# Transposing attention probabilities through DRAM: partition-wise writes and four sorted reads in place of four sorted writes and partition-wide reads

## The chip, the cores and the metric

The kernel is one program on one core of a Trainium2 chip. The metric is the device time of one execution in microseconds, given as the median of several runs. A profiled execution of the same program gives the trace that is read here. The core's engines are named as the profile names them: PE (TensorE; PEld is its weight load), DVE (VectorE), ACT (ScalarE), POOL (GpSimd) and SP (SyncE). DMAs are issued from the queues of SP, ACT and POOL.

## The reference, cut to what matters

All data are 32-bit floats. There are 8 sequences of 128 rows of 512 numbers. Two residual blocks follow one another:

```python
x = x + lora_experts(adapter(x))        # layer 0
x = x + ffn(attention(x, kv_cache))     # layer 1
```

The attention takes most of the work. It has 32 query heads, 8 key heads (4 query heads to each), a head size of 128, and a paged cache of 16 pages of 32 rows for each sequence:

```python
q = rope(rmsnorm(x @ Wq.T)); k = rope(rmsnorm(x @ Wk.T)); v = x @ Wv.T
k_all = concat([k_cache[block_table], k]); v_all = concat([v_cache[block_table], v])
scores = q @ k_all.T * SCALE            # 128 x 640 for each head
scores = where(valid, scores, -1e30)
probs  = softmax(scores)
out    = (probs @ v_all) @ Wo.T
```

The product of probabilities and values needs the probabilities transposed: keys on the partitions, queries along the row. The queries and keys of the scores need a transposition too: the head's 128 numbers on the partitions.

## The kernel before, in words

A unit is one sequence and one key head with its 4 query heads, so there are 64 units, and two neighbouring units (GH = 2) are one step: the same sequence, two key heads. The order on every engine is the order in which the program states the instructions; nothing is rearranged. After a prologue (layer 0, the first projections, tables and rotations) a loop runs `iteration(u)` for u from 0 to 66. Several units are under way in it at once. In iteration u:

- SP gathers the key pages of the next step (`gather`, L196: 32 KB each): 10 in the even iterations, 6 in the odd ones (L1245). The first three stand ahead of the read of exchange u-1 (`exchange_in`), the others behind it.
- POOL gathers values (`gather_v`, L206), and in odd iterations makes the rotation tables of a later step (`make_tables`, L235, two products).
- For each of the 4 heads PE computes the scores (L837, L840), DVE adds the mask and finds the lowest (L850), ACT takes the exponential (L861), DVE the reciprocal of the sum (L866), POOL divides (L867), and DVE turns 32 x 32 blocks of the result into the tile `pb` (`blocks`, L872). At the third head DVE also turns the blocks of queries and keys of unit u+2 into the end of the same tile (`blocks_qk`, L823). PE puts output products (L1044) and projections (L261) of other units between the heads; DVE takes the projections up (L264).
- ACT then copies the queries and keys of unit u+1 out of what exchange u-1 brought (`heads_qk`, L906), takes the squares and scaled values of unit u+3 (`norms`, L310 and L312), and issues its half of the write of exchange u. POOL finishes the norms (L314, L316).
- After the four heads `exchange_out(u)` writes `pb` to DRAM (L886). `exchange_in(u)` reads it back in the next iteration (L896, L899).
- DVE rotates the queries and keys of unit u+3 (`rotate`, L328 to L346). PE multiplies probabilities and values of unit u-2 (`values`, L919).

**The exchange.** `pb` holds, on each of 128 partitions, QD = 4 pieces of XW = 800 numbers: PW = 640 of probabilities and NH * 32 = 160 of queries and keys. The turn of 32 x 32 blocks has transposed within the blocks. What is left is to move block (i, k) to (k, i), where i and k count the four groups of 32 partitions and the four pieces of a row; this goes through the DRAM tile `px`. Before the change the sorting is done by the writes. There are four, one for each group i of 32 partitions, in the order of the groups: the first two on SP's queue, the others on ACT's. Each writes pieces of 3200 bytes to their sorted places. Then two reads on SP's queue bring whole rows of DRAM into all 128 partitions: queries and keys (`qkb`) first, then the probabilities (`pT`). The tile `pb` has one buffer, `pT` two, `qkb` one. Units 0 and 1 use the `pT` buffers for their `pb`, which have no room for queries; those of unit 1 are put into a gap of `xo` and written in four DMAs of their own.

The two halves of the movement, as they stand:

```python
m = dram_x.tile([QD, 32, QD, XW], F32, tag="px", name=f"px_{u}")
...
out=m[:, :, i, n:end].rearrange("k b f -> b k f"),
in_=src[i * 32 : (i + 1) * 32],
...
nc.sync.dma_start(out=qkb, in_=m[:, :, PW:])
...
nc.sync.dma_start(out=pT, in_=m[:, :, :PW])
```

The functions that the diff touches, with what calls them, follow.

Of the kernel before, what the change touches and what calls it, by code (L numbers as in the profile page):

```python
# [9 lines left out]
F32 = mybir.dt.float32  # L10
I32 = mybir.dt.int32
AF = mybir.ActivationFunctionType
# [4 lines left out]
P = 128  # L17
B = 8
S = 128
# [4 lines left out]
D = 128  # L24
HKV, REP = 8, 4
NH = REP + 1
PAGES, PSIZE, NPP = 64, 32, 16
# [3 lines left out]
GH = 2  # L31
NQ = HKV // GH
HW = NH // 2 * D + D
QD = P // 32
HN = DM // 2
PW = REP * (LC + 1) * 32
XW = PW + NH * 32
# [21 lines left out]
def adaln_ffn_kernel(  # L59
# [25 lines left out]
    nc = tc.nc  # L85
# [33 lines left out]
        out=nw, in_=norm_w.rearrange("o (t d) -> o t d", t=2).to_broadcast([P, 2, D])  # L119
# [15 lines left out]
    xo = keep.tile([P, B // 2, 7, 2, S], F32, name="xo")  # L135
# [90 lines left out]
    NU = len(units)  # L226
    rs_t, qk_t, vn_t, tab_t, c_t, part_t = {}, {}, {}, {}, {}, {}

    def make_tables(st):

        b = st % B
        t = pj.tile([P, 2, 4, D // 2], F32, tag="tab", name=f"tab_{st}", bufs=2)
        nwv = nw.rearrange("p i (t d) -> p (i t) d", t=2)
        for i, f in enumerate((cos, sin)):
            nc.gpsimd.tensor_tensor(  # L235
                t[:, i], nwv, f[:, b, :].unsqueeze(1).to_broadcast([P, 4, D // 2]), ALU.mult
            )
        tab_t[st] = t
# [64 lines left out]
    def norms(u):  # L303

        cs, b = c_t[u], units[u][0] % B
        ss = pj.tile([P, NH], F32, tag="ss", name=f"ss_{u}", bufs=5)
        sq = pj.tile([P, D], F32, tag="sq", name=f"sq_{u}")
        for h in range(NH):
            at = h // 2 * HW + h % 2 * D if h < REP else 2 * D
            nc.scalar.activation(sq, cs[:, at : at + D], AF.Square, accum_out=ss[:, h : h + 1])  # L310
        vn = pj.tile([P, D], F32, tag="vn", name=f"vn_{u}", bufs=6)
        nc.scalar.activation(vn, cs[:, 2 * HW - D :], AF.Copy, scale=down[:, b : b + 1])  # L312
        vn_t[u] = vn
        nc.gpsimd.tensor_scalar(ss, ss, 1.0 / D, eps[:, b : b + 1], ALU.mult, ALU.add)  # L314
        rs = pj.tile([P, NH], F32, tag="rs", name=f"rs_{u}", bufs=5)
        nc.gpsimd.tensor_tensor(rs, ss, mhalf, ALU.pow)  # L316
        rs_t[u] = rs
# [31 lines left out]
    def rotate(u):  # L349
        rotate_q(u)  # L350
        rotate_k(u)
# [46 lines left out]
    with ExitStack() as l0:  # L398
# [217 lines left out]
        for t in range(B):  # L616
# [31 lines left out]
                l0_angles(t - 1)  # L648
            if t in (3, 6):
                gather_v(t // 3 - 1, 0, LC)  # L650
            if t in (5, 6):
                make_tables(t - 5)
            if t == 4:
                project_whole(0, 0, 0, 0)
            if t == 5:
# [12 lines left out]
        project_whole(0, 1, 1, 0)  # L668
        l0_turn(B - 2)
        rotate(1)  # L670
        l0_experts(B - 1)
        project_whole(1, 0, 0, 0)
        transpose_qk(1)
# [117 lines left out]
    with ExitStack() as l1:  # L791
# [6 lines left out]
        )  # L798

        p_t, pb_t, pT_t, den_t, o_t, oT_t, y_t = {}, {}, {}, {}, {}, {}, {}  # L800
        mask_t, px_t, qkb_t, qk_out = {}, {}, {}, {}

        def make_mask(st):
            b = st % B
# [4 lines left out]
        def new_pb(u):  # L809

            if u < 2:
                pb_t[u] = wk1.tile([P, QD, PW], F32, tag=f"pT{u}", name=f"pb_{u}")
                return
            pb_t[u] = wk1.tile([P, QD, XW], F32, tag="pb", name=f"pb_{u}")

        def blocks_qk(u, w):

            if w == 1:
                gap = xo[:, 0, 4:].rearrange("p x c s -> p (x c s)")[:, : NH * S]
                qk_out[w] = gap.rearrange("p (i f) -> p i f", i=QD)  # L820
            else:
                qk_out[w] = pb_t[w][:, :, PW:]
            nc.vector.transpose(  # L823
                qk_out[w].rearrange("p i (h a) -> p h i a", a=32),
                qk_t.pop(u).rearrange("p h t d -> p h (t d)").rearrange(
                    "p h (i a) -> p h i a", a=32
                ),
            )
# [40 lines left out]
        def blocks(u, h):  # L869
# [4 lines left out]
                p_t.pop((u, h)).rearrange("p (j i a) -> p j i a", i=QD, a=32),  # L874
            )

        def exchange_out(u):

            pb = pb_t.pop(u)
            m = dram_x.tile([QD, 32, QD, XW], F32, tag="px", name=f"px_{u}")  # L880
            w = XW if u + 2 in range(3, NU) else PW
            for i in range(QD):
                eng = nc.sync if i < QD // 2 else nc.scalar
                for n, end in ((PW, w), (0, PW)) if u == 1 else ((0, w),):
                    src = qk_out[u] if n else pb[:, :, :end]
                    (nc.sync if n else eng).dma_start(  # L886
                        out=m[:, :, i, n:end].rearrange("k b f -> b k f"),
                        in_=src[i * 32 : (i + 1) * 32],
                    )
            px_t[u] = m  # L890

        def exchange_in(u):
            m = px_t.pop(u).rearrange("k b i f -> (k b) i f")
            if u + 2 in range(3, NU):
                qkb = wk1.tile([P, QD, NH * 32], F32, tag="qkb", name=f"qkb_{u + 2}")
                nc.sync.dma_start(out=qkb, in_=m[:, :, PW:])  # L896
                qkb_t[u + 2] = qkb
            pT = wk1.tile([P, QD, PW], F32, tag=f"pT{u % 2}", name=f"pT_{u}")
            nc.sync.dma_start(out=pT, in_=m[:, :, :PW])  # L899
            pT_t[u] = pT  # L900

        def heads_qk(u):

# [321 lines left out]
        def iteration(u):  # L1225
# [16 lines left out]
                slots = (1, 2, 6) if four else (4, 5, 3)  # L1242
            st = u // GH
            pages = on(u) and 1 < st + 1 < NQ * B
            first, end = ((0, 10), (10, NPP))[u % GH]  # L1245
            if pages:
                gather(st + 1, first, first + 3)
            if on(u - 1):
# [266 lines left out]
```

## Time and profile before

| what | value |
|---|---|
| median of 3 runs | 1235.75 us (1232.12 to 1240.6) |
| the profiled execution's own time | 1228.33 us |
| its span in the profile | 1226.5 us |
| DVE, POOL and ACT busy | 909.9, 721.2 and 503.7 us |
| DMA moved in the span | 302.71 MB, 247 GB/s on average |
| L837, scores: matmuls of 128x512 | 504, 259.2 us in all |
| L919, values: matmuls of 128x512 | 640, 295.6 us in all |
| L872, block turns of probabilities | 256, 825 ns each |
| L906, copies of queries and keys | 61, 712 ns each |
| L235, tables | 64 products, 741 to 747 ns each |

How to read the profile: times count from the start of the span. The matmuls of PE are pipelined and overlap, so the sum over a group is more than the time in which the group ran. A line of a timeline gives the start, the time taken, the engine (with a q for an engine's queue that issues DMAs), the line of the program, the operation, what it writes and reads, how many in a row, and in brackets the engine's idle time before it with what ended it. In the table of stages each number of busy us has the count of instructions in brackets behind it. A group's name such as `pT<-px` means: into the tile `pT`, from `px`.

### The profile page before, as it was taken

How to read it: one execution, taken by the hardware profiler on the slowest of the kernel's cores; microseconds unless marked ns; L12 is line 12 of the kernel's file. 1: busy time of each engine (PE TensorE's matmuls, PEld its weight loads, DVE VectorE, ACT ScalarE, POOL GpSimd, SP SyncE). 2: the span in 40 equal slices, each digit the busy share in tenths (PEclk: the TensorE clock that was granted, in tenths of full speed). 3: DMA queues.
4: the chain of work that ended last, by engine and by line, in shares of the span. 5: the costliest groups of instructions: out<-in, count | busy, mean ns of one | idle time of the engine just before them, and what ended most of it. 6: DMA issues, size and time to landing. Idle time of an engine off the chain costs nothing.

```text
span 1226.5 us, 16786 instructions
## 1 busy us (share of the span) xinstructions
PE 1202.6 (98%) x4159; PEld 709.2 (58%) x4159; DVE 909.9 (74%) x2098; ACT 503.7 (41%) x1457; POOL 721.2 (59%) x801
## 2 busy tenths in 40 slices
PE   8999989999999999999999999999999999999998
PEld 7765445565555556555556565655555555655444
DVE  2545877887988787878888787888787878876522
ACT  1344544444444444444344444444443444443211
POOL 2433868778755576677656675687556775732100
PEclk9999999999999999999999999999999999999999
DMA  8832688888888988898789888998889888888742
GB/s 306 286 101 96 205 253 251 247 272 275 261 245 251 280 259 237 294 288 287 236 263 294 281 231 270 297 289 248 246 257 287 262 255 262 263 260 235 219 126 97
DMA packets 206836, 302.71 MB, mean 247 GB/s; under 512 B 84819, under 2 KB 120404, under 8 KB 205844
## 3 DMA queue, kind: packets, MB, share of 16 engines
q1 hardware_dynamic: 174964, 208.72, 53.9%
q10 hardware_dynamic: 18720, 52.32, 15.9%
q0 software_dynamic: 13056, 40.60, 9.8%
q8 instruction: 33, 0.54, 0.2%
q14 instruction: 63, 0.52, 0.1%
HBM read 185.64 MB, written 115.93 MB: 246 GB/s over the span
## 4 chain that ended last, share of the span: by engine, by line
PE 68%; DMA 12%; DVE 6%; POOL 5%; issue 3%; SPq 3%; ACT 2%; ACTq 0%; DVEq 0%; POOLq 0%
PE o L919 15%; PE p L261 14%; PE s L837 12%; PE y L1044 10%; DMA px<-pb 9%; PE s L840 3%; PE bp L548 2%; PE op L1402 2%; DVE pb L872 2%; PE cp L526 2%; PE y L1057 2%; POOL p L867 2%; PE fz L733 2%; PE p L294 2%; POOL wqkv L166 1%
## 5 line engine op out<-in xcount | busy, mean ns | idle before, releaser
L861 ACT ACTIVATE p<-p,low 128x640 f32<-128x640 f32 x256 | 211.6, 827 | 463.1 <-DVE den L866 300.9
L867 POOL TENSOR_SCALAR p<-p,den 128x640 f32<-128x640 f32 x256 | 208.6, 815 | 270.2 <-DVE den L866 268.8
L261 PE MATMUL p<-wqkv,xo 128*128 128x384 f32 x784 | 282.3, 487 | 5.1 <-DVE c L264 4.9
L850 DVE CUSTOM_DVE_ANT_0 p<-s,mask,rs 128x640 f32<-128x640 f32 x256 | 222.0, 878 | 78.8 <-PE s L840 77.9
L837 PE MATMUL s<-kt,qkT 128*128 128x512 f32 x504 | 259.2, 596 | 8.5 <-DVE low L850 3.3
L919 PE MATMUL o<-pT,vt 128*128 128x512 f32 x512 | 230.2, 592 | 0.0
L872 DVE STREAM_TRANSPOSE pb<-p 128x640 f32<-128x640 f32 x256 | 211.0, 825 | 18.7 <-POOL p L867 18.7
L1044 PE MATMUL y<-wo,oT 128*128 128x256 f32 x784 | 206.6, 380 | 0.1
L261 PEld LDWEIGHTS p<-wqkv,xo 128*128 128x128 f32 x784 | 147.8, 190 | 75.9 <-DVE c L264 10.1
L840 PEld LDWEIGHTS s<-qkT 128*128 128x128 f32 x504 | 95.8, 190 | 120.5 <-issue 120.5
L206 POOL DMA_INDIRECT vt<-in_vc,vrow x128 | 143.3, 1120 | 33.8 <-issue 31.8
L919 PEld LDWEIGHTS o<-pT,vt 128*128 128x128 f32 x512 | 97.3, 190 | 110.3 <-issue 95.2
L837 PEld LDWEIGHTS s<-kt,qkT 128*128 128x128 f32 x504 | 93.4, 190 | 82.3 <-issue 34.3
L1044 PEld LDWEIGHTS y<-wo,oT 128*128 128x128 f32 x784 | 131.8, 191 | 8.9 <-PE s L840 0.2
L310 ACT ACTIVATE sq<-c 128x128 f32<-128x128 f32 x320 | 98.8, 309 | 8.1
L840 PE MATMUL s<-qkT 128*128 128x128 f32 x504 | 96.8, 274 | 0.0
L823 DVE STREAM_TRANSPOSE pb<-ca 128x640 f32<-128x640 f32 x60 | 50.3, 839 | 52.5 <-DMA px<-pb 51.5
L316 POOL TENSOR_TENSOR rs<-ss,mhalf 128x5 f32<-128x5 f32 x64 | 83.1, 1298 | 5.3
L942 ACT COPY oT<-o 128x512 f32<-128x512 f32 x64 | 37.5, 585 | 90.7 <-PE o L919 67.4
L919 PE MATMUL o<-pT,vn 128*128 128x512 f32 x128 | 65.4, 592 | 0.0
L314 POOL TENSOR_SCALAR ss<-ss,eps 128x5 f32<-128x5 f32 x64 | 21.6, 338 | 74.2 <-ACT sq L310 74.2
L264 DVE TENSOR_TENSOR c<-c,p 128x384 f32<-128x384 f32 x84 | 44.8, 534 | 22.5 <-PE p L261 22.4
(193 smaller groups left out, 1415.0 us busy)
## 6 DMA issues: line engine op xcount, KB each, us to landing
pT<-px SPq DMA_DIRECT2D x64, 1280.0 KB
px<-pb ACTq DMA_DIRECT2D x120, 400.0 KB
px<-pb SPq DMA_DIRECT2D x120, 400.0 KB
qkb<-px SPq DMA_DIRECT2D x61, 320.0 KB
kt<-in_kc SPq DMA_DIRECT2D x512, 32.0 KB
wqkv<-in_wqkv POOLq DMA_DIRECT2D x32, 384.0 KB, 5.3
wo<-in_wo POOLq DMA_DIRECT2D x17, 512.0 KB, 6.2
yd<-yp SPq DMA_DIRECT2D x12, 512.0 KB
```

The costliest lines, as they stand in the source:

```text
L206: nc.gpsimd.indirect_dma_start(out=kv_t[step][1][:, c, :], out_offset=None, in_=vc, in_offset=bass.IndirectOffsetOnAxis(ap=vrow[:, hf, at ...
L261: nc.tensor.matmul(out=ps, lhsT=xo[:, pr, x, c, :], rhs=w[:, c, :], start=(c == 0), stop=(c == 1))
L310: nc.scalar.activation(sq, cs[:, at : at + D], AF.Square, accum_out=ss[:, h : h + 1])
L316: nc.gpsimd.tensor_tensor(rs, ss, mhalf, ALU.pow)
L837: nc.tensor.matmul(out=s[:, :L], lhsT=qkT[:, h, :], rhs=kt[:, :, g % GH, :], start=True, stop=True)
L840: nc.tensor.matmul(out=s[:, L:NK], lhsT=qkT[:, h, :], rhs=qkT[:, REP, :], start=True, stop=True)
L850: nc.vector.tensor_tensor_reduce(out=p, in0=s_t.pop((u, h))[:, :NK], in1=mask_t[st], scale=rs_t[u][:, h : h + 1], scalar=BIG, op0=ALU.add, ...
L861: nc.scalar.activation(p, p, AF.Exp, bias=low, scale=-1.0, accum_out=den)
L867: nc.gpsimd.tensor_scalar(p_t[u, h], p_t[u, h], den, 1.0, ALU.mult, ALU.mult)
L872: nc.vector.transpose(pb_t[u][:, :, h * w : (h + 1) * w].rearrange("p i (j a) -> p j i a", a=32), p_t.pop((u, h)).rearrange("p (j i a) -> ...
L919: nc.tensor.matmul(out=o, lhsT=vt[:, c, j * D : (j + 1) * D] if c < LC else vn_t.pop(u), rhs=pT[:, c], start=(c == 0), stop=(c == LC),)
L1044: nc.tensor.matmul(out=y_t["y"][:, half * HN : (half + 1) * HN], lhsT=part(key)[:, i * S : (i + 1) * S], rhs=wo_t[:, slot(w, key[0] // (B ...
```

## The change

The writes no longer sort: two DMAs of 64 partitions each, one on SP and one on ACT, write each partition's row in one piece (12,800 bytes). The reads sort instead: four DMAs on SP's queue, one for each piece k of a row, gather that piece from all rows into the 32 partitions of group k, with the queries and keys and the probabilities together. So `qkb` is gone, and `heads_qk` reads the end of the `pT` tile, which grows to XW. Room is made by one buffer instead of two for the tables, with the second table of the prologue made after `rotate(1)`, and by letting the squares of `norms` go into `vn` in place of a tile of their own. Units 0 and 1 now have a full-sized `pb`, so unit 1's queries need no gap in `xo`. The key pages are gathered 8 and 8 instead of 10 and 6.

```diff
-        t = pj.tile([P, 2, 4, D // 2], F32, tag="tab", name=f"tab_{st}", bufs=2)
+        t = pj.tile([P, 2, 4, D // 2], F32, tag="tab", name=f"tab_{st}")
...
-        sq = pj.tile([P, D], F32, tag="sq", name=f"sq_{u}")
+        vn = pj.tile([P, D], F32, tag="vn", name=f"vn_{u}", bufs=6)
         for h in range(NH):
             at = h // 2 * HW + h % 2 * D if h < REP else 2 * D
-            nc.scalar.activation(sq, cs[:, at : at + D], AF.Square, accum_out=ss[:, h : h + 1])
-        vn = pj.tile([P, D], F32, tag="vn", name=f"vn_{u}", bufs=6)
+            nc.scalar.activation(vn, cs[:, at : at + D], AF.Square, accum_out=ss[:, h : h + 1])
...
-            if t in (5, 6):
-                make_tables(t - 5)
+            if t == 5:
+                make_tables(0)
...
         rotate(1)
+        make_tables(1)
         l0_experts(B - 1)
...
-                pb_t[u] = wk1.tile([P, QD, PW], F32, tag=f"pT{u}", name=f"pb_{u}")
+                pb_t[u] = wk1.tile([P, QD, XW], F32, tag=f"pT{u}", name=f"pb_{u}")
...
+        def width(u):
+
+            return XW if u + 2 in range(3, NU) else PW
+
         def exchange_out(u):
 
-            pb = pb_t.pop(u)
-            m = dram_x.tile([QD, 32, QD, XW], F32, tag="px", name=f"px_{u}")
-            w = XW if u + 2 in range(3, NU) else PW
-            for i in range(QD):
-                eng = nc.sync if i < QD // 2 else nc.scalar
-                for n, end in ((PW, w), (0, PW)) if u == 1 else ((0, w),):
-                    src = qk_out[u] if n else pb[:, :, :end]
-                    (nc.sync if n else eng).dma_start(
-                        out=m[:, :, i, n:end].rearrange("k b f -> b k f"),
-                        in_=src[i * 32 : (i + 1) * 32],
-                    )
+            pb, w = pb_t.pop(u), width(u)
+            m = dram_x.tile([P, QD, XW], F32, tag="px", name=f"px_{u}")
+            for eng, at in ((nc.sync, slice(0, P // 2)), (nc.scalar, slice(P // 2, P))):
+                eng.dma_start(out=m[at, :, :w], in_=pb[at, :, :w])
             px_t[u] = m
 
         def exchange_in(u):
-            m = px_t.pop(u).rearrange("k b i f -> (k b) i f")
-            if u + 2 in range(3, NU):
-                qkb = wk1.tile([P, QD, NH * 32], F32, tag="qkb", name=f"qkb_{u + 2}")
-                nc.sync.dma_start(out=qkb, in_=m[:, :, PW:])
-                qkb_t[u + 2] = qkb
-            pT = wk1.tile([P, QD, PW], F32, tag=f"pT{u % 2}", name=f"pT_{u}")
-            nc.sync.dma_start(out=pT, in_=m[:, :, :PW])
-            pT_t[u] = pT
+
+            m, w = px_t.pop(u), width(u)
+            pT = wk1.tile([P, QD, XW], F32, tag=f"pT{u % 2}", name=f"pT_{u}")
+            for k in range(QD):
+                nc.sync.dma_start(
+                    out=pT[k * 32 : (k + 1) * 32, :, :w],
+                    in_=m[:, k, :w].rearrange("(i b) f -> b i f", i=QD),
+                )
+            if w == XW:
+                qkb_t[u + 2] = pT[:, :, PW:]
+            pT_t[u] = pT[:, :, :PW]
...
-            first, end = ((0, 10), (10, NPP))[u % GH]
+            first, end = ((0, 8), (8, NPP))[u % GH]
```

`blocks_qk` now always writes to the end of `pb` (in place of the gap in `xo` for unit 1).

More of the change, by code (lines that the diff above doesn't have):

```diff
@@ L800, in adaln_ffn_kernel @@
         p_t, pb_t, pT_t, den_t, o_t, oT_t, y_t = {}, {}, {}, {}, {}, {}, {}
-        mask_t, px_t, qkb_t, qk_out = {}, {}, {}, {}
+        mask_t, px_t, qkb_t = {}, {}, {}
         def make_mask(st):
@@ L816, in blocks_qk @@
         def blocks_qk(u, w):
[L818 to L822, printed above, removed]
             nc.vector.transpose(
-                qk_out[w].rearrange("p i (h a) -> p h i a", a=32),
+                pb_t[w][:, :, PW:].rearrange("p i (h a) -> p h i a", a=32),
                 qk_t.pop(u).rearrange("p h t d -> p h (t d)").rearrange(
```

## The prediction

> **What bounds the kernel now.** I read the busy table first, then the clock row and the times by stage, then the waits, and last one exchange in order of time.
>
> ```profile
> span 1226.5 us, 16786 instructions
> PE 1202.6 (98%) x4159; PEld 709.2 (58%) x4159; DVE 909.9 (74%) x2098; ACT 503.7 (41%) x1457; POOL 721.2 (59%) x801
> PEclk9999999999999999999999999999999999999999
> ```
>
> TensorE is busy 98% of the span at full clock. So nothing off TensorE shortens the kernel by more than the gaps between matmuls. By stage (length, then busy time of PE, PEld, DVE, ACT and POOL, clock, DMA share, GB/s):
>
> ```profile
> 133.70:1051.90 918.20, 906.93 (x2998) 531.96 (x2998) 746.67 (x1615) 407.38 (x1208) 623.25 (x665) 1.00 0.86 265
> ```
>
> From the first scores of unit 2 (133.7) to those of unit 58 (1051.9) there are 56 units, 918.2 / 56 = **16.4 us a unit**, and TensorE idles only 918.2 - 906.9 = 11.3 us. That is all that a faster exchange can win here. But the DMA engines are 86% busy in the same stage, so a slower exchange can take over. The waits on it are small today:
>
> ```profile
> SPq L886 <- DMA px<-pb: 81.9, 29, 5.0
> ...
> DVE pb L823 <- DMA px<-pb: 51.5, 33, 3.6
> ACT qkT L906 <- DMA qkb<-px: 4.4, 5, 1.9
> ```
>
> The columns are total us, count, longest. ScalarE, which copies queries and keys back (L906), waited for them only 5 times in 61; so the read is just in time. One exchange, that of unit 30, across the engines:
>
> ```profile
> 609.10 0.84 DVE L872 STREAM_TRANSPOSE pb<-p 128x640 f32<-128x640 f32 x1 [0.18 <-POOL p L867]
> ...
> 609.97 0.31 ACTq L886 DMA_DIRECT2D px<-pb  x1
> ...
> 613.42 0.95 SPq L886 DMA_DIRECT2D px<-pb  x2
> ...
> 620.00 0.74 SPq L896 DMA_DIRECT2D qkb<-px  x1
> 620.79 0.62 SPq L899 DMA_DIRECT2D pT<-px  x1
> ...
> 623.74 0.73 ACT L906 COPY qkT<-qkb 128x640 f32<-128x640 f32 x1 [0.18 <-DMA qkb<-px]
> ...
> 627.97 1.09 PE L837 MATMUL s<-kt,qkT 128*128 128x512 f32 x2
> ```
>
> Call T the end of the last block transpose (609.94). The writes are complete at 619.6 (the trace's semaphore records), T + 9.7, because SP's pair went out 3.5 us late, held by a semaphore that ACT's write was still using. The 320 KB of queries, read first, are in 3.7 us after their issue; probabilities follow until 627.28. The copy ends at 624.47, and the scores that need it start 3.5 us later. **That 3.5 us is the slack of the exchange.**
>
> **How fast the pieces move.** Four stretches of the same view (last column GB/s):
>
> ```profile
> 611.00:613.00 2.00, 2.00 (x9) 1.36 (x8) 1.47 (x5) 0.53 (x1) 1.81 (x2) 1.00 0.97 202
> 623.50:625.50 2.00, 2.00 (x7) 0.91 (x6) 1.91 (x5) 1.76 (x8) 0.75 (x2) 1.00 1.02 403
> 628.00:629.50 1.50, 1.50 (x7) 1.00 (x7) 0.97 (x4) 0.59 (x1) 1.31 (x2) 1.00 1.04 414
> ```
>
> In the first only ACT's writes run, from partitions 64 to 127, 32 at a time: 202 GB/s with the engines 97% "busy". In the second pT is read back into all 128 partitions: 403. In the third SP writes from the lower half and ACT from the upper: 414. So one half of the partitions alone gets half the rate, whatever the queue. The packets were 3200, 2560 and 3200 bytes; size is not what differs.
>
> [...]
>
> **The change, part by part.**
>
> *Writes.* Two DMAs of 64 partitions in place of four of 32, the same 1,638 kB, the halves as before on SP and ACT. Larger pieces win nothing at 414 GB/s: 1638 / 414 = 4.0 us if both start together. With 0.6 us to start and 0.6 to close (ACT's packets at 610.5 and 615.0, landing at 615.68) and some other traffic that is about T + 6. One half alone: ACT's pair of unit 30 took 609.97 to 615.68 = 5.7; with one issue less, **5.6**. Each queue issues one write less (0.33 to 0.36 us). SP's 3.5 us wait I expect to go, as the odd iterations, with three pages between read and write, do not have it (SP's write of unit 31 went out at 626.47 with T at 626.44). This is a real gain, T + 9.7 to T + 6.
>
> *Reads.* Four DMAs, in SP's order: into partitions 0-31, 32-63, 64-95, 96-127, queries and probabilities together. Old read: 620.00 to 627.28 = 7.3 (unit 31: 6.9) for 1,638 kB, so 2.9 to 3.3 beyond 1638 / 403 = 4.1; about 1.0 of it is the ramp in 640-byte pieces, which goes. New: between 1638 / 403 + 2.1 = **6.2** if writing into a quarter is not slowed, and 1638 / 202 + 2.1 = **10.2** if it is. I take 10.2: the nearest row is a quarter's write at 202, one queue serves the four in turn, and the first two lie on one half. And queries are no longer first: L906 waits for all four. So the queries are there 10.2 us after the issue instead of 3.7. SP's two more issues (4 for 2, some 0.35 each against 0.54 and 0.62) cost SP nothing visible: they go out while the first streams.
>
> *The loop that this closes.* On ACT the queue of iteration u holds: copy of queries (L906, exchange u-1), norms of unit u+3 (L310, L312), then its half of the write of exchange u. So a late read delays the next write. Where L906 last waited, at 410.25, ACT's write went out at 412.68:
>
> ```profile
> 410.25 0.72 ACT L906 COPY qkT<-qkb 128x640 f32<-128x640 f32 x1 [1.45 <-DMA qkb<-px]
> ...
> 412.68 0.31 ACTq L886 DMA_DIRECT2D px<-pb  x1
> ```
>
> From read to read: 2.43 (copy and norms) + 5.6 (ACT's half; SP's is done by then) + 0.25 from landing to SP's issue (0.16 to 0.39 at 634.10 and 620.00) + 10.2 = **18.5 us, over 16.4**. With 6.2 it is 14.5 and does not bind. Is it entered? Undelayed, a read lands at T + 6 + 0.25 + 10.2 = T + 16.5, some 0.1 us after the next T on average (T moves on by 16.4), hence ACT's next write is 2.5 us late, and it grows until scores wait: scores of u+2 start 0.95 us after the landing (copy 0.73, handover). Behind L906 also stand the power on POOL (L316), the rotation on VectorE (L342) and the next mask (L850); in this stage VectorE is busy 746.7 / 56 = 13.3 us a unit, so it keeps pace with 18.5.
>
> *The sum.* The read of exchange 0 (320 x 4 kB, half rate) keeps SP's queue until about 142, so exchange 1 is written at 146.7 and read by 156.8; scores 3 move from 151.3 to 157.8. Exchange 2 is read by 156.8 + 18.5 = 175.3 (before, its write could start at 150.6). Then 54 rounds of 18.5 to exchange 56: 1174.3, scores of 58 at 1175.3 instead of 1051.9: **+123 us**. From there the units are as long as the loop (18.4 us mean for 58 to 62), and I leave the tail's 174.6. Span 1350; the profiled execution's own time was 1228.33 on 1226.5, so 1352. That execution lies 0.6% below the median of the runs, 1235.75, so on the median's footing **1360**. Half a us in the round is 27 us.
>
> *Edits at nothing.* Squares go into vn before its copy (L310, L312): same engine, same order. Tables in one buffer: L235 now waits for the rotation of the unit before; in iteration 31 it ran at 614.82, after that rotation (613.27 + 0.49), so the wait is already over; behind it on POOL stands L867, which needs a mask and an exponential first. Uncovered it would be 2 x 0.74 = 1.5 us every second unit. The moved second table (POOL, 1.5 us) fits between POOL's weight issues (until 109.55) and rotate(2) at 110.92: 0.1 late, at most 1.5, once. Pages 8 and 8 instead of 10 and 6: the same 16 issues of some 0.85 us; SP issues five after the read in 4.3 us, long before the next T; the odd iteration's, which the next scores need, land just behind the read, some 0.6 after, under the 0.95 of the copy. The four writes from xo for unit 1 (SP, 0.43 to 1.78 us each) go: inside the start, -1 to 0.
>
> **Rivals.**
> - *Not slower: SBUF takes a quarter at full rate.* Round 14.5; TensorE stays the bound. For: no row of this trace shows it slowed. [...] Of the 11.3 us of gaps perhaps half go: 1223 on the profile's footing, 1230 on the median's; between 1224 and 1236. It decides where the round is 16.4, a read of 8.1 us or 273 GB/s.
> - *Half slowed:* engines run on from the lower half into the upper so the stream overlaps. Read 8.6, round 16.9: +35, near 1270. Against: in 611 to 614.5 two such transfers in a row held 200 GB/s.
> - *SP's half also waits for ACT's*, as at 613.42: 4 us more a round, 22.5: near 1580.
>
> **Chances.** Main 0.70 (own range 1315 to 1425, rounds of 17.7 to 19.7); full rate 0.16; half slowed 0.10; SP's wait 0.04. About 1% is what a measurement of this kernel can tell from no change. Of the full-rate case 0.04 is faster by over 1% and 0.12 within; of half slowed 0.02 is within. So faster 0.04, same 0.14, slower 0.82. The range 1240 to 1460 leaves out the full-rate case and SP's wait.
>
> **What would show it.** Right: stretches of the four reads near 200 GB/s; L906 waiting for pT<-px in nearly every unit; gaps of PE before L837 released by qkT; PE near 88%; rounds near 18.5. Wrong: reads near 400 GB/s; SPq L886 still waiting (then the write's gain is not there either); gaps of PE ended by something other than L906, which would put the loss in VectorE's or POOL's order.

## The result and the profile after

The change makes the kernel **slower: 1443.79 us (1441.93 to 1445.33) against 1235.75 us (1228.88 to 1240.6), five runs each; ratio 1.169, 95% interval 1.165 to 1.174**. The profiled execution has a span of 1440.2 us, 213.7 more than before. In the program after, the line numbers are smaller, most of them by five: L901 is the copy of queries and keys (L906 before), L881 the two writes (L886), L889 the four sorted reads, L832 the scores against cached keys (L837), L818 the turn of queries and keys into `pb` (L823), L341 the rotation (L342), L313 and L315 the norms on POOL (L314 and L316), L311 the scaled values on ACT (L312).

The busy table, the clock row and the two lines of the chain that ended last:

```profile
span 1440.2 us, 16867 instructions
...
PE 1273.9 (88%) x4159; PEld 735.1 (51%) x4159; DVE 911.0 (63%) x2098; ACT 515.4 (36%) x1457; POOL 705.3 (49%) x801
...
PEclk9999899999999999999998999999999999999999
...
DMA 50%; PE 15%; ACT 14%; SPq 7%; DVE 6%; issue 4%; POOL 3%; ACTq 0%; POOLq 0%; DVEq 0%
DMA pT<-px 33%; DMA px<-pb 14%; ACT vn L310 8%; SPq L889 5%; ACT p L856 3%; ACT qkT L901 3%; POOL rs L315 2%; PE bp L547 2%; DMA kt<-in_kc 2%; PE op L1397 2%; DVE p L845 2%; PE cp L525 2%; PE o L914 1%; PE p L294 1%; PE y L1052 1%
```

PE was busy 98% of the span and is busy 88%. The largest parts of the chain are the members of the loop that the prediction wrote down: sorted reads, writes, the copy and the norms between them on ACT, and SP's issues of the reads. The stage from the first scores of unit 2 to those of unit 58, in the columns used before (length, then PE, PEld, DVE, ACT, POOL, clock, DMA share, GB/s):

```profile
134.62:1256.39 1121.77, 976.82 (x2998) 558.34 (x2997) 748.29 (x1616) 416.14 (x1202) 607.44 (x662) 0.94 0.96 217
```

That is 1121.8 / 56 = 20.0 us a unit instead of 16.4, and 204.5 of the 213.7 us are lost by the scores of unit 58. The DMA engines are busy 96% instead of 86% while they move 217 GB/s instead of 265. The waits on the exchange, and those behind them (before, the copy waited 5 times and the turn into `pb` 33 times):

```profile
POOL ss L313 <- ACT vn L310: 372.9, 63, 12.5
DVE ca L341 <- POOL rs L315: 281.7, 59, 7.6
ACT qkT L901 <- DMA pT<-px: 277.9, 51, 11.3
...
PEld s L832 <- ACT qkT L901: 131.1, 33, 10.6
...
DVE pb L818 <- DMA px<-pb: 8.9, 11, 1.6
```

ACT's copy waits for the reads in 51 of 61 units (5 before), the norms, the power and the rotation queue up behind it, and the scores wait for the copy. The waits of SP's queue:

```profile
SPq L889 <- DMA px<-pb: 281.6, 69, 7.2
SPq L881 <- DMA pT<-px: 125.8, 60, 3.5
```

So the reads wait for a write, ACT's, and SP's own half waits for the reads of the exchange before: at 513.76 it went out 0.06 us after the third of them had landed, whose completion semaphore it uses. (A completion semaphore is the counter that the trace's record of a DMA's landing names; in the traces of the kernels before and after, all DMAs of SP and ACT use the same eight of them, and this write waited until the DMA before it on the same one had landed.) The wait is off the loop, since SP's half still lands 4.9 us ahead of ACT's there. One round, first ACT's lines, then SP's:

```profile
495.67 0.73 ACT L901 COPY qkT<-pT 128x640 f32<-128x640 f32 x1 [5.80 <-DMA pT<-px]
...
498.48 0.47 ACTq L881 DMA_DIRECT2D px<-pb  x1
...
515.84 0.73 ACT L901 COPY qkT<-pT 128x640 f32<-128x640 f32 x1 [5.92 <-DMA pT<-px]
...
518.66 0.45 ACTq L881 DMA_DIRECT2D px<-pb  x1
```

```profile
495.71 0.45 SPq L881 DMA_DIRECT2D px<-pb  x1
...
505.62 1.76 SPq L889 DMA_DIRECT2D pT<-px  x4
...
513.76 0.47 SPq L881 DMA_DIRECT2D px<-pb  x1
...
524.47 1.76 SPq L889 DMA_DIRECT2D pT<-px  x4
```

Copy at 495.67; ACT's half goes out 2.81 us later, after the norms; the reads go out at 505.62, when it has landed; the next copy comes 10.22 us after that. Two stretches of the same unit, in the columns of the stage:

```profile
507.00:515.00 8.00, 6.16 (x18) 2.84 (x16) 7.13 (x14) 0.92 (x2) 2.93 (x4) 1.00 1.03 212
520.00:523.50 3.50, 3.50 (x12) 2.08 (x11) 3.12 (x8) 0.74 (x2) 2.98 (x4) 0.84 0.87 178
```

The four sorted reads run at 212 GB/s with a DMA share of 1.03. In the second stretch, just after TensorE had idled 3.46 us (ahead of its matmul at 516.62), its clock is 0.84.

**A table for what follows.** For each kernel, means over units 3 to 54 of its trace, in us. "Written" is from T (end of the last block transpose) to the landing of the last write; "read" from the first issue to the last landing; "copy" counts from the start of ACT's copy, which itself takes 0.73; two units are always the first column plus "T to scores of u+2".

| kernel | scores of u to T | T to written | read | copy to scores of u+2 | T to scores of u+2 | unit |
|---|---|---|---|---|---|---|
| before | 15.0 | 9.2 | 7.5 | (queries early) | 17.7 | 16.4 |
| after | 16.5 | 11.6 | 10.4 | 1.2 | 23.4 | 19.9 |
| one write on SP | 15.8 | 6.3 | 11.5 | 1.8 | 20.0 | 17.9 |
| one write on SP, queries first | 14.9 | 7.2 | 11.0 | (queries early) | 19.6 | 17.2 |
| before, queries last | 16.2 | 10.1 | 7.6 | 1.6 | 19.4 | 17.8 |
| after, unsorted reads | 16.5 | 10.3 | 7.0 | 2.0 | 19.5 | 18.0 |

### The profile page after: what moved, and what is told of

It reads as the page before. It is cut to its first block, busy times and chain, and to the rows that moved or that the text cites. A ratio compares the mean times of both kernels' runs of the same rounds, so it can differ in the third digit from the quotient of the medians.

```text
span 1440.2 us, 16867 instructions
## 1 busy us (share of the span) xinstructions
PE 1273.9 (88%) x4159; PEld 735.1 (51%) x4159; DVE 911.0 (63%) x2098; ACT 515.4 (36%) x1457; POOL 705.3 (49%) x801
## 4 chain that ended last, share of the span: by engine, by line
DMA 50%; PE 15%; ACT 14%; SPq 7%; DVE 6%; issue 4%; POOL 3%; ACTq 0%; POOLq 0%; DVEq 0%
DMA pT<-px 33%; DMA px<-pb 14%; ACT vn L310 8%; SPq L889 5%; ACT p L856 3%; ACT qkT L901 3%; POOL rs L315 2%; PE bp L547 2%; DMA kt<-in_kc 2%; PE op L1397 2%; DVE p L845 2%; PE cp L525 2%; PE o L914 1%; PE p L294 1%; PE y L1052 1%
## 5 line engine op out<-in xcount | busy, mean ns | idle before, releaser
L832 PE MATMUL s<-kt,qkT 128*128 128x512 f32 x504 | 296.0, 672 | 151.1 <-ACT qkT L901 103.3
L261 PE MATMUL p<-wqkv,xo 128*128 128x384 f32 x784 | 281.2, 487 | 1.2 <-POOL wqkv L166 1.2
L1039 PE MATMUL y<-wo,oT 128*128 128x256 f32 x784 | 227.5, 411 | 2.4 <-POOL wo L989 2.4
L832 PEld LDWEIGHTS s<-kt,qkT 128*128 128x128 f32 x504 | 97.2, 208 | 248.5 <-ACT qkT L901 131.1
L341 DVE SCALAR_TENSOR_TENSOR ca<-c,rs,tab 128x128 f32<-128x128 f32 x64 | 22.5, 351 | 281.7 <-POOL rs L315 281.7
L313 POOL TENSOR_SCALAR ss<-ss,eps 128x5 f32<-128x5 f32 x64 | 17.6, 275 | 372.9 <-ACT vn L310 372.9
L261 PEld LDWEIGHTS p<-wqkv,xo 128*128 128x128 f32 x784 | 148.3, 190 | 71.0 <-POOL wqkv L166 3.6
L835 PEld LDWEIGHTS s<-qkT 128*128 128x128 f32 x504 | 105.0, 208 | 139.2 <-issue 139.2
L901 ACT COPY qkT<-pT 128x640 f32<-128x640 f32 x61 | 44.3, 726 | 328.7 <-DMA pT<-px 277.9
L1039 PEld LDWEIGHTS y<-wo,oT 128*128 128x128 f32 x784 | 145.4, 210 | 14.9 <-POOL wo L989 3.0
L835 PE MATMUL s<-qkT 128*128 128x128 f32 x504 | 103.7, 290 | 0.0
L310 ACT ACTIVATE vn<-c 128x128 f32<-128x128 f32 x320 | 99.3, 310 | 8.1
L315 POOL TENSOR_TENSOR rs<-ss,mhalf 128x5 f32<-128x5 f32 x64 | 76.7, 1198 | 5.3
L1108 DVE TENSOR_TENSOR yp<-yp,y 128x512 f32<-128x512 f32 (+3 forms) x94 | 60.1, 640 | 0.0
```

What stands on the lines that cost most here:

```text
L261: nc.tensor.matmul(out=ps, lhsT=xo[:, pr, x, c, :], rhs=w[:, c, :], start=(c == 0), stop=(c == 1))
L310: nc.scalar.activation(vn, cs[:, at : at + D], AF.Square, accum_out=ss[:, h : h + 1])
L832: nc.tensor.matmul(out=s[:, :L], lhsT=qkT[:, h, :], rhs=kt[:, :, g % GH, :], start=True, stop=True)
L835: nc.tensor.matmul(out=s[:, L:NK], lhsT=qkT[:, h, :], rhs=qkT[:, REP, :], start=True, stop=True)
L1039: nc.tensor.matmul(out=y_t["y"][:, half * HN : (half + 1) * HN], lhsT=part(key)[:, i * S : (i + 1) * S], rhs=wo_t[:, slot(w, key[0] // (B ...
```

## The experiments

**1. The moves by themselves.** No layers and no other engines: each form of write and read, one after the other.

```python
sp.dma_start(out=m[halves[0]], in_=t[halves[0]])
act.dma_start(out=m[halves[1]], in_=t[halves[1]])
...
sp.dma_start(out=m, in_=t)
...
sp.dma_start(out=t[:, k, :], in_=m[:, k, :])
```

> Only DMAs between one SBUF tile (128 x 4 x 800 floats) and one DRAM tile of the same size, one kind after another, nothing beside them; all of the layers is left out, so only the durations from first issue to last landing count. [...] Open, both ends given: reads 0,1 on SP with 2,3 on ACT between 6 (halves overlap) and 10 (they do not). Writes: two halves on SP and ACT about 8 if the queues do not overlap, as at the start of the changed kernel (129.08 to 136.9), 6 if they do; four quarters about 6; one DMA over 128 partitions about 5.5.

Measured, from first issue to last landing (semaphore records of the trace), 1,638 kB each:

| move | us |
|---|---|
| two halves, SP and ACT | 9.1 and 9.0 |
| four writes of 32 partitions, two on SP, two on ACT | 6.5 and 6.4 |
| one write of 128 partitions, SP | 5.2 and 5.2 |
| four sorted reads, SP, order 0 1 2 3 | 9.6 |
| the same in order 0 2 1 3 | 9.1 |
| the same on two queues | 7.7 |
| whole rows into 32 partitions, four times | 9.4 |
| piece k of each row into 128 partitions, four times | 6.7 |
| the two reads of before | 6.9 |

Stretches of it (length, DVE, POOL, clock, DMA share, GB/s): two halves, sorted reads, four writes, pieces into 128 partitions, one write:

```profile
5.50:12.00 6.50, 0.00 (x0) 0.00 (x0) 1.00 0.97 215
15.00:22.00 7.00, 0.00 (x0) 0.00 (x0) 1.00 1.01 222
24.50:29.00 4.50, 0.00 (x0) 0.00 (x0) 1.00 0.83 313
31.50:36.00 4.50, 0.06 (x1) 0.00 (x0) 1.00 0.91 345
38.00:41.50 3.50, 0.00 (x0) 0.00 (x0) 1.00 0.97 410
```

These are times of a single execution. Two things follow. The half rate of the sorted reads belongs to the 32 partitions they go into, not to gathering in DRAM: whole rows into 32 partitions are as slow (9.4), and the same pieces into 128 are not (6.7). And the two halves do **not** run side by side. Both were issued at 4.22; ACT's landed at 9.98 and SP's at 13.32, and in the packet records SP's first packet starts at 9.42, when ACT's are all but done (9.62). Of the four smaller writes one of each queue landed at 27.46 and 27.63, the others at 29.66 and 29.87: those share. One DMA over all 128 partitions was the fastest of the writes (5.2). Why the two halves take turns and the four smaller writes do not, no run here tells.

**2. Queries first.** In the kernel after, each sorted read in two, those of the queries ahead.

```diff
-            for k in range(QD):
-                nc.sync.dma_start(
-                    out=pT[k * 32 : (k + 1) * 32, :, :w],
-                    in_=m[:, k, :w].rearrange("(i b) f -> b i f", i=QD),
-                )
+            for n, end in ((PW, w), (0, PW)):
+                for k in range(QD if end > n else 0):
+                    nc.sync.dma_start(
+                        out=pT[k * 32 : (k + 1) * 32, :, n:end],
+                        in_=m[:, k, n:end].rearrange("(i b) f -> b i f", i=QD),
+                    )
```

> The changed kernel, but each sorted read is cut in two and the four small reads of queries and keys (160 of 800 numbers) go first. The bytes and the partition groups stay. My theory (the round is bound by what the copy L906 waits for): the small reads land after 2.1 + 328 kB at 200 GB/s = 3.7 to 4.5 us instead of 10.4, so the round falls from 20 to 13.5 or 14, below TensorE's 16.4, and the time falls to 1235 to 1275 (SP issues four DMAs more a unit, and the key pages still land behind all eight reads, which may cost up to 0.5 us a unit). Rival (the load on the DMA engines as a whole is what costs, 1.6 MB at half rate in each unit): little changes, 1420 to 1450. If the copy still waits for all eight reads: 1440 to 1470.

1505.9 us, ratio 1.217 (1.210 to 1.225): missed. The copy does come early now, 5.2 us ahead of the last landing on average, but SP's half went to wait:

```profile
SPq L881 <- DMA px<-pb: 305.6, 46, 9.8
```

ACT's half of one unit was issued at 533.39 and landed at 539.12; SP's went out at 539.18. The trace's records show the same completion semaphore for both, as in 44 of the 54 units 3 to 56 of this run; in the kernel after the two halves have different ones in all 54. Behind SP's half stand the key pages, for which the scores then wait (157.4 us, against none of note). It is the third rival of the prediction, brought in by the experiment; so this run doesn't say what queries last cost.

**3. Four writes.** The kernel after with four writes of 32 partitions, whole rows.

```diff
-            for eng, at in ((nc.sync, slice(0, P // 2)), (nc.scalar, slice(P // 2, P))):
+            for i in range(QD):
+                eng, at = nc.sync if i < QD // 2 else nc.scalar, slice(i * 32, (i + 1) * 32)
```

> The changed kernel with four writes of 32 partitions (two on SP, two on ACT) in place of two of 64; rows stay in one piece, the reads stay. If ACT's write is late in odd rounds because the engines finish SP's one DMA first (7.2 against 5.7 us from issue to landing), smaller DMAs let the queues take turns: 0 to 1.4 us less in every second round, 27 rounds, so 1405 to 1444. If it is the size of the pieces (12,800 bytes) that keeps the queues from taking turns: no change, 1444 within 10.

1428.87 us, ratio 1.153 (1.147 to 1.159): 15 us better. Written at T + 11.2 instead of 11.6, unit 19.7. By itself this form saved 2.6 us; here little, and not in the odd rounds, where it was expected: ACT's pair takes 7.3 us there as ACT's half did (7.2), and 5.4 instead of 5.7 in the even ones. SP's pair goes out 3.0 (odd) and 4.8 us (even) ahead of ACT's, so there is little left to share.

**4. ACT's write ahead of its copy.**

```diff
-            if u + 1 in range(3, NU):
-                heads_qk(u + 1)
...
-            if u < 2:
-                norms(4 + u)
-            elif 5 < u + 3 < NU:
-                norms(u + 3)
...
                 exchange_out(u)
+            if u + 1 in range(3, NU):
+                heads_qk(u + 1)
+            if u < 2:
+                norms(4 + u)
+            elif 5 < u + 3 < NU:
+                norms(u + 3)
```

> The changed kernel with ACT's write of exchange u moved ahead of the copy L901 and the norms in ACT's order, so a late read no longer delays the next write through ACT. My theory (a round through ACT's order): the round becomes two units for T to T: scores to T 15 to 17, write 8, read 10.4, copy 0.95, so 34.4 to 36.4 for two units, 17.2 to 18.2 a unit, and the time 1295 to 1350. Rival (the read's length alone costs, whatever ACT's order): 1430 to 1450. A second rival (norms now later, so that POOL's power and VectorE's rotation set the round): 1370 to 1420.

1507.22 us, ratio 1.216 (1.209 to 1.223): missed, by the same clash. ACT's half landed at 538.11, SP's half went out at 538.17:

```profile
SPq L881 <- DMA px<-pb: 308.2, 44, 10.9
```

Both halves have the same completion semaphore in 42 of the 54 units. With both in a row, a unit takes 21.1 us. Inconclusive for the order on ACT; the next run takes the write off ACT's queue altogether.

**5. One write.** The kernel after, the write in one DMA of 128 partitions on SP.

```diff
-            for eng, at in ((nc.sync, slice(0, P // 2)), (nc.scalar, slice(P // 2, P))):
-                eng.dma_start(out=m[at, :, :w], in_=pb[at, :, :w])
+            nc.sync.dma_start(out=m[:, :, :w], in_=pb[:, :, :w])
```

> The kernel after, with one write of all 128 partitions on SP in place of the two halves on SP and ACT; the four sorted reads stay. Theory (the round is copy and norms 2.8, ACT's half of the write 6.5, issue 0.1, sorted reads 10.4, and it is too long because the write stands in ACT's order and moves at half rate): ACT issues no write any more, so the late copy of queries no longer delays the write; the whole write took 5.2 us by itself. Scores of u+2 then start 5.2 + 0.15 + 10.4 + 0.95 = 16.7 us after the last block transpose of u, about one unit of 16.4: TensorE binds again or nearly, 16.4 to 17.0 us a unit, 1236 to 1280 us in all, and the reads stay at 10.4. Rival (the sorted reads at half rate are the whole loss, wherever the write stands): 1420 to 1444 us. Rival (the whole write gains only its own 1.3 us on ACT's half): round 18.6, near 1370.

1318.75 us, ratio 1.067 (1.062 to 1.072). The write goes out at T + 0.05 and has landed at T + 6.3, not 11.6: **the writes' place in ACT's order, behind a copy that waits, and the two halves in a row are together worth 125 us.** This run does not tell the two apart. The time is above what I expected, for two reasons in the table: among the other transfers the write took 6.3 and the reads 11.5, not 5.2 and 10.4, and behind the late copy stand norms, power and rotation, so that every second unit's scores start 2.8 us after the start of the copy, and the others 0.8 (L900 is the copy in this program):

```profile
POOL ss L313 <- ACT vn L310: 258.0, 63, 12.5
...
DVE ca L341 <- POOL rs L315: 174.5, 54, 6.8
...
ACT qkT L900 <- DMA pT<-px: 137.0, 44, 6.0
...
PEld s L832 <- DVE low L845: 55.4, 42, 3.2
```

**6. One write, and queries first** (experiments 5 and 2 together).

> The same single write on SP, and the four sorted reads split in two sets, four of the queries first and four of the probabilities after them. With no write on ACT the small set can't delay a write, as it did in the run with queries first and two halves. Theory: the queries are there some 4 to 5 us after the first issue, so the scores have 5 us of slack; TensorE binds at 16.4 us a unit: 1225 to 1250 us. Rival (the sorted reads' 10.4 us on SP's queue bind whatever is first, through the pages that stand behind them): 1300 us or more, with scores waiting for key pages.

1273.34 us, ratio 1.029 (1.024 to 1.035). The scores no longer wait for queries. A unit takes 17.2 us, the DMA engines are 92% busy, and TensorE idles 46 us in the stage instead of 11. In the whole run it waited 36.9 us for key pages:

```profile
133.90:1099.39 965.49, 919.84 (x2998) 539.21 (x2997) 750.66 (x1621) 416.64 (x1209) 620.18 (x667) 0.98 0.92 252
```

```profile
PE s L832 <- DMA kt<-in_kc: 36.9, 16, 6.3
```

The read of one exchange has landed at T + 18.4, later than the next T, so the next write has to share with it (written at T + 7.2 instead of 6.3), and the key pages stand behind both on the same queue. So this exchange costs about 38 us more than the one before the change even when nothing waits for the queries, and 49 us against experiment 7, which has the same other edits. How much of that is the reads' half rate and how much the crowded queue, no run here divides.

**7. The other edits alone.** The kernel before with one buffer for tables, the second table later, squares into `vn`, pages 8 and 8.

```diff
-        t = pj.tile([P, 2, 4, D // 2], F32, tag="tab", name=f"tab_{st}", bufs=2)
+        t = pj.tile([P, 2, 4, D // 2], F32, tag="tab", name=f"tab_{st}")
...
-            first, end = ((0, 10), (10, NPP))[u % GH]
+            first, end = ((0, 8), (8, NPP))[u % GH]
```

> The kernel before with everything of the change but the exchange: one buffer for the tables, the second table made later, squares into vn, eight and eight pages. Theory: these cost nothing, 1236 within 6 us. Rival (a part of the loss is theirs, by the table's buffer on POOL or the pages' place on SP's queue): 1245 us or more, with POOL or key pages ending gaps of TensorE.

1224.36 us, ratio **0.991** (0.989 to 0.994): a small gain where I had put nothing. Experiments 10 and 11 divide it.

**8. Queries last.** The kernel before with its two reads swapped, at full rate.

```diff
+            pT = wk1.tile([P, QD, PW], F32, tag=f"pT{u % 2}", name=f"pT_{u}")
+            nc.sync.dma_start(out=pT, in_=m[:, :, :PW])
+            pT_t[u] = pT
             if u + 2 in range(3, NU):
...
-            pT = wk1.tile([P, QD, PW], F32, tag=f"pT{u % 2}", name=f"pT_{u}")
-            nc.sync.dma_start(out=pT, in_=m[:, :, :PW])
-            pT_t[u] = pT
```

> The kernel before with only its two reads swapped: probabilities first, queries last, both at full rate into 128 partitions. It takes from the change the one part that queries come last, without half rate in the reads. Theory (what sets the time is the round from read to read through L906, norms and ACT's write): queries are there 6.9 us after the issue, not 3.7; round 2.8 + (ACT's pair 5.7, or 9.7 if SP's pair still waits for a semaphore of ACT's) + 0.3 + 6.9 = 15.7 or 19.7; so 1236 to 1260 without SP's wait and 1400 to 1440 with it. Rival (the order of the reads doesn't matter, only their rate): 1236 within 6 us.

1313.99 us, ratio 1.061 (1.056 to 1.067): **75 to 79 us for the order alone** (by the ratio and by the medians).

```profile
ACT qkT L906 <- DMA qkb<-px: 174.4, 59, 5.4
```

Neither of my two numbers came: SP's wait did not come back, but ACT's pair took more than 5.7. In one round the copy is at 505.58, ACT's pair goes out at 508.00 and lands at 515.36, the reads go out at 515.49 and land at 522.95: 2.4 + 7.4 + 0.1 + 7.5 = 17.4.

**9. Unsorted reads.** The kernel after, piece k of each row into all partitions. The sort between groups of partitions is left out, so the result is that of an unsorted exchange.

```diff
-                    out=pT[k * 32 : (k + 1) * 32, :, :w],
-                    in_=m[:, k, :w].rearrange("(i b) f -> b i f", i=QD),
+                    out=pT[:, k, :w],
+                    in_=m[:, k, :w],
```

> The kernel after, whose four reads take piece k of every row into all 128 partitions, instead of piece k of each row's place into 32 partitions: the same four issues and bytes, queries still last, but the sort between partitions is left out, so the numbers are those of an unsorted exchange. It takes away the half rate of the reads alone. Theory (half rate costs 3.7 us in every round): round 0.1 + 2.8 + 6.5 + 0.1 + 6.7 to 7.6 = 16.2 to 17.1, about 1240 to 1290 us. Rival (the order alone is the loss, as with queries last at full rate, where the round was 17.8): near 1314 us, and the half rate is then worth the difference to 1444. Rival (the rate is not what costs): 1420 to 1444 us.

1321.98 us, ratio 1.072 (1.069 to 1.074). The reads take 7.0 instead of 10.4, so **the half rate of the reads is worth 122 us here**, and what stays is near experiment 8. The theory's 1240 to 1290 missed because both halves now go out almost together in every second unit and then stand in line (ACT's half takes 9.3 us in the odd units and 6.5 in the even ones):

```profile
529.03 0.72 ACT L901 COPY qkT<-pT 128x640 f32<-128x640 f32 x1 [0.70 <-DMA pT<-px]
...
531.80 0.46 SPq L881 DMA_DIRECT2D px<-pb  x1
...
531.84 0.46 ACTq L881 DMA_DIRECT2D px<-pb  x1
...
543.15 0.84 DVE L818 STREAM_TRANSPOSE pb<-ca 128x640 f32<-128x640 f32 x1 [2.63 <-DMA px<-pb]
...
543.26 1.76 SPq L889 DMA_DIRECT2D pT<-px  x4
```

SP's half landed at 537.54, ACT's at 543.12: 5.7 and then 5.6 us. DVE, which wants `pb` for the next queries, waits for it as well.

**10 and 11. Pages alone, and the other small edits alone**, each on the kernel before: only `((0, 8), (8, NPP))`; and experiment 7 with `((0, 10), (10, NPP))`.

> The kernel before with eight and eight key pages in place of ten and six, nothing else. All edits but the exchange together gave 0.991 of the time before. Theory: the even share of pages brings it, since it takes two issues and two pages out of the turn in which SP's write is late: 0.990 to 0.994. Rival: it is the tables or the squares, then 1.000 within 0.003.

> The kernel before with one buffer for the tables, the second table made later and the squares into vn, pages ten and six as before. Theory: nothing, 1.000 within 0.003. Rival: the gain of all edits together is theirs, 0.991.

Pages 8 and 8: 1223.4 us, ratio **0.993** (0.990 to 0.995). The rest with 10 and 6: 1242.75 us, ratio **1.008** (1.006 to 1.011). The wait of L823 for the tile `pb`, 51.5 us before, in the first and in the second:

```profile
DVE pb L823 <- DMA px<-pb: 9.5, 10, 1.6
```

```profile
DVE pb L823 <- DMA px<-pb: 73.3, 36, 5.6
```

With equal turns the exchange's write leaves `pb` earlier (T + 8.5 instead of 9.2), DVE is not held there, and PE waits less for DVE's take-up of projections (ahead of L261: 2.6 us in all instead of 15.1). Why the tables and the squares cost 0.8% with ten pages, and with eight nothing that shows beside experiment 10, is not shown by a run of its own. The traces fit the squares: with them in `vn` ACT's write leaves later (next part), at T + 0.37 instead of 0.13 on average in the even units, and with ten pages SP's pair waits there for a completion semaphore of ACT's and follows at T + 3.8 instead of 3.5; with eight pages (experiment 7) it leaves there at T + 0.05.

**12. Pages between queries and probabilities.** Experiment 6, with five key pages moved in between (part 0 of `exchange_in` reads the queries, part 1 the probabilities).

```diff
-                exchange_in(u - 1)
+                exchange_in(u - 1, 0)
             if pages:
                 gather(st + 1, first + 3, end)
+            if on(u - 1):
+                exchange_in(u - 1, 1)
```

> One write of all 128 partitions on SP and queries read first, as in the run that came to 1273 us, with the five key pages that stand behind all eight sorted reads put between the four of the queries and the four of the probabilities. Nothing is left out. Theory (what is left of the loss there is key pages that come late, because they stand on SP's queue behind a read at half rate): scores no longer wait for key pages, TensorE binds again, 1225 to 1245 us. Rival (the DMA engines, busy 92% there, are the bound whatever the order): 1260 us or more.

1451.69 us, ratio 1.176 (1.173 to 1.179): missed widely. SP's queue (L898 the queries, L890 the probabilities, L880 the write):

```profile
604.98 1.75 SPq L898 DMA_DIRECT2D pT<-px  x4
607.26 3.75 SPq L196 DMA_DIRECT2D kt<-in_kc  x5
611.06 1.84 SPq L890 DMA_DIRECT2D pT<-px  x4
613.00 0.37 SPq L880 DMA_DIRECT2D px<-pb  x1
...
624.41 2.44 SPq L898 DMA_DIRECT2D pT<-px  x4
```

Queries were in at 608.46, pages at 613.80, probabilities at 619.75, the write at 624.32: one after the other, 3.6 + 5.3 + 6.0 + 4.6 = 19.5 us from write to write. The pages' issues of 0.85 us each used to go out while the reads streamed; here nothing streams meanwhile but the pages. DVE waits for `pb` in 59 units (277.0 us). My theory was wrong, and of the rival only the number came, not its reason: the order does matter, by 178 us between this run and experiment 6, which had the better one.

## Why the prediction was right, and where its sizes were off

**The mechanism is the one predicted.** The loop of copy, norms, ACT's half and reads replaced TensorE as the bound. Its signs were named ahead and came: reads near 200 GB/s (212), L901 waiting for `pT<-px` in nearly every unit (51 of 61), PE at 88%. Experiments 5 and 9 each take one member out of the loop, the write in ACT's order and the half rate, and leave 1319 and 1322; experiment 8 puts queries last, and nothing else, into the kernel before and makes it 1314; 5 with queries first leaves 1273. The three single effects (125, 122 and 75 to 79 us) can't be added up to the 208 lost. The first two shorten the unit of 19.9 us by 2.0 and 1.9; both together would bring it below TensorE's 16.4, where nothing more is gained, and the third is measured on another kernel.

**The size.** Predicted 1360, measured 1444: above the 1315 to 1425 of the main case and its rounds of 17.7 to 19.7, within 1240 to 1460. Span 1440.2 against 1350: 54 rounds of 19.95 instead of 18.5 are +78, the tail 183.8 instead of 174.6 is +9, and exchange 2 was read by 177.6 instead of 175.3, +2; sum 90. The round by its terms (means of exchanges 3 to 56):

| term | predicted | measured |
|---|---|---|
| copy and norms to ACT's write | 2.43 | 0.09 + 2.81 |
| ACT's half | 5.6 | 6.47 |
| landing to SP's issue | 0.25 | 0.14 |
| four sorted reads | 10.2 | 10.44 |
| round | 18.5 | 19.95 |

- *The reads* were right: half rate for 32 partitions, which before no row of the trace showed for this direction. The step to it from the 202 GB/s of the writes was an estimate; the runs showed 212 GB/s, and 9.6 against 6.7 us alone.
- *The write, predicted as a real gain from T + 9.7 to T + 6, was a loss*, to T + 11.6, and this is the step that failed. (T + 6 was meant for a write that nothing delays; T + 11.6 is 5.1 until ACT's half goes out, behind the late copy as predicted, and 6.47 for the half itself, against 5.6. That term is worth 0.87 us a round, some 47 us.) I took the 414 GB/s of four 32-partition DMAs for two of 64, which no row of the trace before showed. Alone, both halves took 9.1 us, at 215 GB/s (experiment 1): 1638 / 202 = 8.1, by the rate of one half in the kernel before, and 1 to start and close. ACT's half took 5.7 us in the even rounds, as predicted, and 7.2 in the odd ones, in which SP's half still stood ahead of it: in the round of 498.48 ACT's first packet starts at 500.55, when SP's last ones are under way (until 501.55).
- *Copy to write* is 0.38 longer, some 21 us in 54 rounds, and this comes from an edit that the prediction put at nothing ("same engine, same order"): the squares into `vn`. Before, ACT's write goes out 0.07 us after the last square has started, ahead of the scaled values (L312); with the squares in `vn` the scaled values start only 0.44 after it, and the write with them. In the kernel before:

```profile
412.61 0.31 ACT L310 ACTIVATE sq<-c 128x128 f32<-128x128 f32 x1
412.68 0.31 ACTq L886 DMA_DIRECT2D px<-pb  x1
...
412.92 0.39 ACT L312 ACTIVATE vn<-c,down 128x128 f32<-128x128 f32 x1
```

In the kernel after:

```profile
518.22 0.31 ACT L310 ACTIVATE vn<-c 128x128 f32<-128x128 f32 x1
...
518.65 0.40 ACT L311 ACTIVATE vn<-c,down 128x128 f32<-128x128 f32 x1
518.66 0.45 ACTq L881 DMA_DIRECT2D px<-pb  x1
```

The scaled values start 0.31 us after the last square in all 64 units of the kernel before and of experiments 8 and 10, and 0.43 or 0.44 after it in all 64 of every kernel whose squares go into `vn` (the kernel after, and experiments 7 and 11, which have the old exchange). That the engine waits there for the squares to leave the tile it overwrites fits, but is not shown apart.
- *Edits at nothing* was wrong for the pages too: 8 and 8 gains 0.7% on the kernel before. I had only counted issues on SP, and not followed the write that they delay to `pb`, to L823 and to PE.
- *The rival at full rate was mispriced.* Experiment 9 has full-rate reads and takes 1322, not 1230: its round of 14.5 had the same 5.6 for ACT's half (6.5 and 9.3 in experiment 9), the same 2.43 from copy to write (2.8 to 2.9) and 6.2 for the reads (7.0).
- *SP's half waiting for ACT's*, given 0.04, did not happen, but experiments 2 and 4 fell into it by four more DMAs or another order, at 1506 and 1507. Which DMAs share a semaphore was not foreseen for any of these kernels, so that the change itself escaped it was in part luck.

**The version that beats both** is the kernel before with pages 8 and 8 (0.993), or with all small edits (0.991); their intervals overlap. Of the forms tried, the exchange is better left as it was. Sorted reads on two queues, which took 7.7 instead of 9.6 us alone, were not tried in the kernel.

## What to carry to other kernels

A sort between groups of partitions cuts a transfer into pieces of 32 partitions; here the pieces moved faster on two queues, one half of the partitions each, than on one queue in turn (7.7 against 9.6 us for the sorted reads by themselves). What the next step needs first should be its own small, early read. Before a transfer is put behind or ahead of another, write down the round that closes over the queues, which here issued in the program's order (SP's lines in experiment 12); an engine that both waits for a read and issues the next write makes one. A bandwidth seen for one shape of DMA was not that of another shape on the same queues (414 GB/s for writes of 32 partitions in the kernel before, 215 for two of 64 in experiment 1): time the shape by itself.

## What the runs showed of the hardware that was not expected

- Two DMAs of 64 partitions on two queues followed one another (5.7 and then 5.6 us, though issued 0.04 us apart, in experiment 9), while DMAs of 32 partitions on the same two queues shared (6.5 us for all four, in experiment 1).
- The sorted reads on two queues, one half of the partitions each, took 7.7 us instead of 9.6 (experiment 1).
- The scaled values on ACT started 0.43 to 0.44 us after the last square where they overwrite its tile, 0.31 where they do not; the earliest DMA issue behind them moved from 0.06 or 0.07 to 0.44 us after that square.
- The granted clock was lower behind TensorE's gaps: 0.84 in the stretch behind a gap of 3.46 us, 0.94 over the stage (1.00 before), and PE's busy time in the stage was 976.8 us instead of 906.9 with the same work. It set no pace here, as far as the waits show: in each of the units 3 to 56 ACT's half goes out at least 1.76 us after T, so the round does not wait for the scores.
- Which transfers share a completion semaphore changed with the number or the order of DMAs elsewhere: the two halves of one write shared one in none of 54 units of the kernel after, in 44 of experiment 2 and in 42 of experiment 4, where one half waited for the other (1506 and 1507 us).
